# Two pairs of images in turn: the pieces of the front, the blocks of bins, and six buffers of head weights

## The chip, the cores and the metric

The kernel runs on one core of a Trainium2 chip. A core has five engines that each work through a queue of their own: PE (matrix products), DVE (VectorE), ACT (ScalarE), POOL (GpSimd) and SP, which here only issues transfers; 16 DMA engines move the data. The metric is the device time of one launch in microseconds (us), as a median over runs.

## The reference, cut to what matters

The input has 4 images of 48 x 48 positions and 128 channels. The first layer (a selective scan) is untouched by the change. The second layer is a spectral attention block; its input x1 is the first layer's output, and per image there are T = 48 tokens of 48 x 128 pixels.

```
xa_n = inorm(gn(x1))                       # group norm, then a norm per token
q, k, v = fno(xa_n; wQ), fno(xa_n; wK), fno(xa_n; wV)    # spectral convolution + skip, 32 heads
attn = softmax(q k^T / c)                  # per image and head: 48 x 48
out  = attn v                              # per head
projd = fno(out; wP)                       # spectral convolution + skip over the 32 heads
attention = inorm(projd + xa)
m = two more spectral layers on inorm(attention)
x = x1 + inorm(m) + attention
```

The kernel works with spectra: the value and the projection weights of a head are multiplied into one complex weight per bin and head, so that `attn v` and the projection become, for each block of bins, a sum over heads h and tokens s of attn[h, t, s] * (weight[h, bin] * spectrum[s, bin]). A complex product is made of three real ones (c = 0, 1, 2).

## The kernel before, in words

The instructions are laid on the engines' queues by a scheduler when the program is built. Those issued through the object `on` keep their program order on their engine (they all carry line 50 in the profile, the helper's line); those issued through `nc` may be moved where their data and buffers allow. A pool of tiles with `bufs=n` gives a tag n buffers in turn; a tile waits until the last reader of the buffer's previous tile is done. Pools that are closed give their memory to later ones.

The front of layer 1 handles the four images as two pairs. Per pair there are: `statistics` (12 `bn_stats`, two aggregates, then `group_affine`, a chain of small operations over DVE, PE and ACT); `first_norm`, a generator that yields after each piece (sums over positions with matmuls into `pm`, a normed image into `xa`, its square `sq`, and sums of squares with matmuls into `pv`); and `forward_w`, a generator that makes the transform along the width, six pieces of two matmuls `pa`, two evacuations to `a` and a store to DRAM (`da_x`). Before, pair 0 goes through all of it, then pair 1. Then come the combined head weights: `gw` on DVE, 12 steps of three transposes (`pgt`) into a PSUM bank and an ACT copy into `gtt`, and four stores into the DRAM tensor `dgt`. After that the spectra `a2` are read back and scaled, and `xa` is transposed (`pxn`).

The middle makes scores and softmax, and writes the tokens' spectra to the DRAM tensor `dxt` (`keys`).

The block loop follows. For each pair and each block k of 384 bins there are three accumulators in PSUM (`acc`, one set), and 12 groups (q, g): q counts 16 tokens, g counts 8 heads. A group takes `xrep` (spectra of 16 tokens, replicated over 8 heads, two transfers of 576 KB, new at each q, two buffers) and `grep` (weights of 8 heads, replicated over 16 tokens, one transfer of 576 KB, four per block, four buffers). ACT copies two thirds of `grep` to PSUM (line 1371), DVE multiplies it with `xrep` (line 1373), POOL multiplies the last third (line 1377), and PE sums with the attention weights `attn_c` (line 1381). At the end of a block ACT copies one accumulator (`s1`, line 1389), three DVE operations make `zt` (lines 1392 to 1394), and eight transposes (`pz`, line 1399) with two ACT copies write it to `z2`. Ahead of the loop stand 11 small loads of `wpv` and `mask`, four tiles `e_w` on DVE, and for each pair 48 matmuls (`pa`, line 1340) and a copy that give `a0_bd`, which is used only in the tail.

Of the kernel before, what the change touches and what calls it, by code (L numbers as in the profile page):

```python
# [10 lines left out]
F32 = mybir.dt.float32  # L11
# [4 lines left out]
PSUM = bass.MemoryType.PSUM  # L16
# [3 lines left out]
B, T, H, W = 4, 48, 48, 128  # L20
# [9 lines left out]
NH = 32  # L30
# [5 lines left out]
class Ordered:  # L36


    def __init__(self, tc):
        for name in ("tensor", "vector", "scalar", "gpsimd"):  # L40
            setattr(self, name, _OrderedEngine(tc, getattr(tc.nc, name)))
# [693 lines left out]
def layer1(ctx, tc, io, x1_dram, out):  # L735
# [5 lines left out]
    nc = tc.nc  # L741
# [10 lines left out]
    on = Ordered(tc)  # L752
# [48 lines left out]
    def statistics(psum, p, x):  # L801

        mv = small.tile([128, 2, 2], F32, tag=f"mv{p}", name=f"mv{p}", bufs=1)
        for b in range(2):
            st = small.tile([128, 6, 6], F32, tag="st", name=f"st1_{p}_{b}")
            for q in range(6):
                on.vector.bn_stats(st[:, q], x[:, b, q * HB : (q + 1) * HB].rearrange("p h t -> p (h t)"))
            on.vector.bn_aggr(mv[:, b], st)
        aff = small.tile([128, 2, 2], F32, tag=f"aff{p}", name=f"aff{p}", bufs=1)
        group_affine(on, small, psum, gmat, eps, mv[:, :, 0], mv[:, :, 1], aff[:, 0], aff[:, 1], 2, f"l1{p}")  # L810
        return aff

    def forward_w(psum, work, p, x, aff):


        da = dram.tile([2, 33, H, 96], F32, name=f"da_x{p}")
        fwa = work.tile([128, 2, 66], F32, tag="fwa", name=f"fwa{p}")
        for b in range(2):
            on.vector.tensor_scalar(fwa[:, b], fw, aff[:, 0, b : b + 1], None, ALU.mult)
        pb = psum.tile([128, 512], F32, tag="mm", name=f"pfwb{p}")  # L820
        on.tensor.matmul(pb[0:66, 0:2], fw, aff[:, 1], start=True, stop=True)
        fwb = small.tile([66, 2], F32, tag="fwb", name=f"fwb{p}")
        on.scalar.copy(fwb, pb[0:66, 0:2])
        for q in range(0, H, HB):
            a = work.tile([66, HB, 2, T], F32, tag="a", name=f"a_{p}_{q}")
# [12 lines left out]
        yield da  # L838

    def first_norm(psum, work, p, x, aff, y):  # L840
# [7 lines left out]
        def spread(t, name, more=False):  # L848

            v = small.tile([128, T], F32, tag="in_s", name=f"in_{name}{p}")  # L850
            on.vector.tensor_reduce(v, t[:, 0 : HB * T].rearrange("p (h t) -> p t h", t=T), AX.X, ALU.add)
            o = psum.tile([128, 512], F32, tag="st", name=f"po_{name}{p}", bufs=2)
            for b in range(2):
# [7 lines left out]

        pm = psum.tile([128, 512], F32, tag="st", name=f"pm{p}", bufs=2)
        for q in range(0, 24, HB):
# [15 lines left out]
        yield  # L879
        pv = psum.tile([128, 512], F32, tag="st", name=f"pv{p}", bufs=2)  # L880
        for i, b, h in quarters:
# [8 lines left out]
            )  # L890
            sq = work.tile([128, 24, T], F32, tag="sq", name=f"sq{p}_{i}")
            on.scalar.activation(sq, d, AF.Square)
# [25 lines left out]

    attn_c = pm.tile([128, B, 4, 3, 64], F32, name="attn_c")
    dxt = dram.tile([B, 4, T, 3 * NC], F32, name="dxt")  # L920

# [50 lines left out]
    def products():  # L972
# [5 lines left out]
        with ExitStack() as pw:  # L978
            q1 = pw.enter_context(tc.tile_pool(name="l1_v1", bufs=1))
            ps_t = pw.enter_context(tc.tile_pool(name="l1_vt", bufs=2, space=PSUM))  # L980

# [77 lines left out]
    with ExitStack() as ph:  # L1059
# [4 lines left out]
        rs, das = [], []  # L1064
        for p in range(2):
            aff = statistics(psst, p, x_in[p])
            norm = first_norm(psst, work, p, x_in[p], aff, xa)
            trans = forward_w(psum, work, p, x_in[p], aff)
            next(norm)
            next(trans)  # L1070
            next(norm)
            for _ in range(5):
                next(trans)
                next(norm)
            das.append(next(trans))
            rs.append(next(norm))
        with ExitStack() as pw:
            ps_t = pw.enter_context(tc.tile_pool(name="l1_wt", bufs=2, space=PSUM))
            q1 = pw.enter_context(tc.tile_pool(name="l1_w1", bufs=1, side="right"))
# [28 lines left out]
            for k in range(4):  # L1108
                gt = q1.tile([NH, 3, NC], F32, name=f"gtt{k}")
                for c in range(3):  # L1110
# [16 lines left out]
        for p in range(2):  # L1127
# [8 lines left out]

            p0 = psst.tile([128, 512], F32, tag="st", name=f"p0_x{p}", bufs=2)
            on.tensor.matmul(p0[0:H, 0:96], over_h, a2p[0:H, 0], start=True, stop=True)
# [48 lines left out]
        f32 = load("f32", [96, 24], io["c_F32"])  # L1187
        pu = psst.tile([128, 512], F32, tag="st", name="pu", bufs=2)
        nc.tensor.matmul(pu[0:24, 0:BT], f32, a2[:, 32], start=True, stop=True)
# [118 lines left out]
    with ExitStack() as ph:  # L1308
        p1 = ph.enter_context(tc.tile_pool(name="l1_q1", bufs=1))
        p2 = ph.enter_context(tc.tile_pool(name="l1_q2", bufs=2))  # L1310
        pg = ph.enter_context(tc.tile_pool(name="l1_qg", bufs=4))
        ps_t = ph.enter_context(tc.tile_pool(name="l1_qt", bufs=1, space=PSUM))
        ps_g = ph.enter_context(tc.tile_pool(name="l1_qp", bufs=2, space=PSUM))
        ps_y = ph.enter_context(tc.tile_pool(name="l1_qy", bufs=1, space=PSUM))


        wpv = p1.tile([128, 2, 4], F32, name="wpv")
        mask = p1.tile([128, 3, T], F32, name="mask")
        for c, n in enumerate(("wPs", "wVs")):
            w = io[n].rearrange("a b -> (a b)")  # L1320
            for g in range(4):
                nc.sync.dma_start(wpv[:, c, g : g + 1], w[8 * g : 8 * g + 8][None].to_broadcast([16, 8]))
        for q in range(3):
            nc.sync.dma_start(
                mask[:, q], io["c_ident"][16 * q : 16 * q + 16, 0:T][:, None].to_broadcast([16, 8, T])
            )
        nc.vector.tensor_mul(wpv[:, 0], wpv[:, 0], wpv[:, 1])
        e_w = []
        for g in range(4):
# [3 lines left out]
            e_w.append(e)  # L1333
        for pair in range(2):
            p = ps_t.tile([128, 512], F32, tag="tr", name=f"pa0{pair}")
# [12 lines left out]
            nc.scalar.copy(a0_bd[:, pair], p[0:96, 0:96])  # L1348
        for pair in range(2):
            for k in range(4):  # L1350
                acc = [ps_y.tile([128, 512], F32, tag=f"acc{c}", name=f"acc{pair}_{k}_{c}") for c in range(3)]
                gr = []
                for q in range(3):
                    x = p2.tile([128, 2, 3, NC], F32, tag="xrep", name=f"xrep{pair}_{k}_{q}")
                    for b in range(2):
                        nc.sync.dma_start(
                            x[:, b].rearrange("p c n -> p (c n)"),
                            dxt[2 * pair + b, k, q * 16 : q * 16 + 16][:, None].to_broadcast([16, 8, 3 * NC]),
                        )
                    for g in range(4):  # L1360
                        t = f"{pair}_{k}_{q}_{g}"
                        if q == 0:
                            r = pg.tile([128, 3, NC], F32, tag="grep", name=f"grep{t}")
                            nc.sync.dma_start(
                                r.rearrange("p c n -> p (c n)"),
                                dgt[k, 8 * g : 8 * g + 8][None].to_broadcast([16, 8, 3 * NC]),
                            )
                            gr.append(r)
                        r = gr[g]
                        gp = ps_g.tile([128, 2, 512], F32, tag="gp", name=f"gp{t}")  # L1370
# [8 lines left out]
                        for c in range(3):  # L1379
                            for b in range(2):  # L1380
# [6 lines left out]
                                )  # L1387
                s1 = p2.tile([128, NC], F32, tag="s1", name=f"s1{pair}_{k}")
                nc.scalar.copy(s1, acc[0][:, 0:NC])  # L1389
# [5 lines left out]
                for k4 in range(2):  # L1395
                    p = ps_t.tile([128, 512], F32, tag="tr", name=f"pz{pair}_{k}_{k4}")
                    for i in range(4):
# [6 lines left out]
                        p[0:96].rearrange("p (k b t) -> p k b t", b=2, t=64)[:, :, :, 0:T],  # L1404
                    )
    mid.close()

# [554 lines left out]
```

## Time and profile before

| | us |
|---|---|
| three runs | 5015.16, 5021.46, 5022.86; median 5021.46 |
| the profiled execution, time | 5017.78 |
| its span | 5016.0 |
| mean granted PE clock | 0.933 |

| stretch of the span | us | what runs in it |
|---|---|---|
| 0 to 4206 | 4206 | the first layer |
| 4206 to 4310 | 104 | the front of layer 1 |
| 4310 to 4445 | 135 | selection, scores, softmax, keys |
| 4445 to 4477.6 | 33 | entry of the block loop |
| 4477.6 to 4745 | 267 | the block loop, 8 blocks |
| 4745 to 5016 | 271 | the two spectral layers of the tail |

How to read it: the stretches are cut from the timeline of one execution, at the first `bn_stats` of layer 1 (4206.53), the last score matmuls, the first `acc` matmul (4477.62) and the last copies to `z2` (4744.45). The profile gives busy times of the engines in any stretch, the idle time before an instruction with the event that ended it, and a chain of waits followed back from the end. Matmul records come in pairs here: one issued product shows as two records or more.

### The profile page before, as it was taken

The numbers are of one execution on the slowest core, as the hardware profiler recorded it, in microseconds if no ns is written. First come the engines' busy times: TensorE is split into PE (matmuls) and PEld (weight loads), VectorE is DVE, ScalarE is ACT, GpSimd is POOL, SyncE is SP. The second block draws the span as 40 slices with busy tenths as digits, with TensorE's granted clock in tenths as the row PEclk, the third lists the DMA queues.
The fourth block names the chain that finished last, engine by engine and source line by source line (L and its number), as shares of the span: only waits on it lengthen the run. The fifth ranks groups of instructions, "written<-read, shape, count | busy, mean of one in ns | idle before, by whom it ended". The sixth has DMA issues, their size and how long they took to land.

```text
span 5016.0 us, 44268 instructions
## 1 busy us (share of the span) xinstructions
PE 4181.6 (83%) x12444; PEld 1916.5 (38%) x12444; DVE 4170.1 (83%) x2901; ACT 2953.2 (59%) x6608; POOL 3993.4 (80%) x2188
## 2 busy tenths in 40 slices
PE   6889898888798988887989888877788787888786
PEld 3334333333343333333433333333333332544443
DVE  3689998989899989898999898988999985556536
ACT  3666566766566666666666666665767663323334
POOL 4589998988899989898999898888999983246531
PEclk9989999999899999998999999998999998989877
DMA  2223232322232333232323332334333323147636
GB/s 54 74 89 101 91 116 89 104 89 97 92 107 94 116 89 104 88 102 90 106 95 117 92 102 91 98 101 96 106 106 102 103 91 88 40 97 172 160 99 151
DMA packets 278691, 501.01 MB, mean 100 GB/s; under 512 B 105940, under 2 KB 190036, under 8 KB 277868
## 3 DMA queue, kind: packets, MB, share of 16 engines
q1 hardware_dynamic: 272864, 495.11, 33.5%
q10 hardware_dynamic: 5580, 3.08, 0.2%
q8 instruction: 98, 1.61, 0.1%
q14 instruction: 149, 1.22, 0.1%
HBM read 462.93 MB, written 35.38 MB: 99 GB/s over the span
## 4 chain that ended last, share of the span: by engine, by line
DVE 17%; PE 15%; ACT 7%; issue 7%; POOL 3%; DMA 3%; SPq 1%; DVEq 0%; POOLq 0%; ACTq 0%
DVE h L50 12%; PE yp L50 4%; ACT da L50 3%; DVE db L50 3%; PE acc L1381 2%; POOL v L1377 1%; DMA grep<-dgt 1%; ACT L50 1%; PE sc L1254 1%; PE pi_p L50 1%; POOL db L50 1%; ACT dt L50 1%; POOL hc L50 1%; DVE m L50 1%; PE pe_m L50 0%
## 5 line engine op out<-in xcount | busy, mean ns | idle before, releaser
L50 POOL TENSOR_TENSOR hc<-h,cbc 128x960 f32<-128x960 f32 (+1 forms) x1280 | 2716.8, 2137 | 443.4 <-DVE h L50 328.5
L50 DVE TENSOR_TENSOR_SCAN h<-da,carry,db 128x961 f32<-128x961 f32 (+1 forms) x1280 | 2702.9, 2130 | 167.4 <-ACT carry L50 108.2
L50 ACT ACTIVATE da<-dt,a_neg 128x480 f32<-128x480 f32 (+1 forms) x2560 | 1660.9, 649 | 1188.1 <-DVE h L50 1143.2
L50 PE MATMUL yp<-hc,ident 128*128 128x480 f32 (+1 forms) x5120 | 2256.9, 568 | 19.4 <-POOL hc L50 19.2
L50 PEld LDWEIGHTS yp<-hc,ident 128*128 128x128 f32 x5120 | 999.1, 197 | 1381.4 <-issue 1003.7
L50 DVE TENSOR_TENSOR db<-du,pb 128x960 f32<-128x960 f32 (+1 forms) x960 | 1064.1, 1108 | 227.9 <-PE pb L50 172.0
L50 POOL TENSOR_TENSOR db<-du,bbc 128x960 f32<-128x960 f32 (+1 forms) x320 | 688.2, 2151 | 18.4 <-DMA bbc<-cd 9.6
L50 PE MATMUL pb<-bs,pick 112*128 112x480 bf16 (+1 forms) x960 | 357.7, 373 | 362.0 <-DVE db L50 360.3
L50 PE MATMUL pc<-pad,cdiag 128*128 128x480 f32 (+1 forms) x630 | 285.2, 564 | 8.3 <-ACT pad L50 8.3
L1377 POOL TENSOR_TENSOR v<-grep,xrep 128x768 f32<-128x768 f32 x96 | 174.4, 1819 | 117.9 <-PE acc L1381 60.8
L1381 PE MATMUL acc<-v,attn_c 128*64 128x384 f32 x1152 | 218.2, 513 | 36.5 <-ACT s L1389 32.1
L1373 DVE TENSOR_TENSOR v<-gp,xrep 128x1536 f32<-128x1536 f32 x96 | 168.1, 1757 | 88.7 <-PE acc L1381 41.3
L50 ACT COPY db<-carry 128x1 f32<-128x1 f32 x1280 | 226.0, 177 | 21.6 <-POOL db L50 15.1
L50 POOL TENSOR_TENSOR du<-dt,xc 128x480 f32<-128x480 f32 (+1 forms) x160 | 204.3, 1277 | 37.0 <-ACT dt L50 37.0
L50 PE MATMUL px<-xc,w_xp 128*112 128x480 f32 (+1 forms) x320 | 214.0, 756 | 16.9 <-ACT xc L50 13.3
L50 PEld LDWEIGHTS <-pick 112*128 112x128 bf16 x960 | 97.6, 102 | 329.1 <-issue 305.9
L50 ACT ACT_TABLE_LOAD x148 | 189.9, 1283 | 42.8 <-PE gv_l L50 19.5
L50 PE MATMUL pd<-xd,w_dt 8*128 8x480 f32 (+1 forms) x320 | 167.5, 603 | 40.5 <-ACT bs L50 24.7
L50 ACT COPY carry<-h 128x2 f32<-128x2 f32 x1024 | 192.6, 188 | 0.0
L50 PEld LDWEIGHTS pc<-pad,cdiag 128*128 128x128 f32 x630 | 122.6, 195 | 142.0 <-issue 115.5
L1371 ACT COPY gp<-grep 128x768 f32<-128x768 f32 x96 | 77.0, 803 | 157.3 <-DVE v L1373 79.7
L50 PE MATMUL yp<-y,ident 128*128 128x480 f32 (+1 forms) x240 | 167.6, 829 | 0.2
(366 smaller groups left out, 3162.5 us busy)
## 6 DMA issues: line engine op xcount, KB each, us to landing
cbc<-cd SPq DMA_DIRECT2D x512, 480.0 KB
bbc<-cd SPq DMA_DIRECT2D x256, 240.0 KB
cbc<-cd SPq DMA_DIRECT2D x128, 384.0 KB
xrep<-dxt SPq DMA_DIRECT2D x48, 576.0 KB
grep<-dgt SPq DMA_DIRECT2D x32, 576.0 KB
bbc<-cd SPq DMA_DIRECT2D x64, 192.0 KB
x<-in_xT SPq DMA_DIRECT2D x16, 288.0 KB
xr<-in_xT SPq DMA_DIRECT2D x16, 288.0 KB
```

The costliest lines, as they stand in the source:

```text
L50: return lambda *args, **kw: self._tc.keep_in_program_order(emit(*args, **kw))
L1254: nc.tensor.matmul(sc[64 * b : 64 * b + 64, g, 0 : 8 * T], qs[:, j, n, 2 * pair + b], f[b][:, 8 * g : 8 * g + 8], start=(jn == 0), stop=False,
L1371: nc.scalar.copy(gp[:, :, 0:NC], r[:, 0:2])
L1373: nc.vector.tensor_mul(v, gp[:, None, :, 0:NC].to_broadcast([128, 2, 2, NC]), x[:, :, 0:2])
L1377: nc.gpsimd.tensor_mul(v3, r[:, 2:3].to_broadcast([128, 2, NC]), x[:, :, 2])
L1381: nc.tensor.matmul(acc[c][64 * b : 64 * b + 64, 0:NC], attn_c[:, 2 * pair + b, g, q], v[:, b, c] if c < 2 else v3[:, b], start=first, stop ...
```

## The change

It has two halves, and some moves of memory.

In the front, statistics of both pairs are made first; those of pair 0 (`bn_stats` and aggregates) are issued through `nc`, so that they may be moved, while those of pair 1 keep their place. Then pieces of both pairs are issued in turn, pair 1 two pieces behind. The tags `a` and `sq` get three buffers, the tag `st` in PSUM three for two; to make room the pool of the transposed weights gets one bank for two, and `gtt` two buffers for four.

In the loop, blocks go k outside, pair inside, so that the weights of a block serve both pairs: 16 loads of `grep` for 32. They get six buffers. All loads of the loop go through `on.sync`, so SP sends them in program order, one step ahead. The loads of `wpv` and `mask` move ahead of the front. The mix of images of a pair moves into the loop, after block 1 of that pair.

```diff
-        for name in ("tensor", "vector", "scalar", "gpsimd"):
+        for name in ("tensor", "vector", "scalar", "gpsimd", "sync"):
...
-                on.vector.bn_stats(st[:, q], x[:, b, q * HB : (q + 1) * HB].rearrange("p h t -> p (h t)"))
-            on.vector.bn_aggr(mv[:, b], st)
+                (on if p else nc).vector.bn_stats(st[:, q], x[:, b, q * HB : (q + 1) * HB].rearrange("p h t -> p (h t)"))
+            (on if p else nc).vector.bn_aggr(mv[:, b], st)
...
-        for p in range(2):
-            aff = statistics(psst, p, x_in[p])
-            norm = first_norm(psst, work, p, x_in[p], aff, xa)
-            trans = forward_w(psum, work, p, x_in[p], aff)
-            next(norm)
-            next(trans)
-            next(norm)
-            for _ in range(5):
-                next(trans)
-                next(norm)
-            das.append(next(trans))
-            rs.append(next(norm))
+        affs = [statistics(psst, p, x_in[p]) for p in range(2)]
+        norms = [first_norm(psst, work, p, x_in[p], affs[p], xa) for p in range(2)]
+        trans = [forward_w(psum, work, p, x_in[p], affs[p]) for p in range(2)]
+        for i in range(9):
+            for p in range(2):
+                if 0 <= i - 2 * p < 7:
+                    if i - 2 * p == 0:
+                        next(norms[p])
+                    if i - 2 * p == 6:
+                        das.append(next(trans[p]))
+                        rs.append(next(norms[p]))
+                    else:
+                        next(trans[p])
+                        next(norms[p])
...
-            ps_t = pw.enter_context(tc.tile_pool(name="l1_wt", bufs=2, space=PSUM))
+            ps_t = pw.enter_context(tc.tile_pool(name="l1_wt", bufs=1, space=PSUM))
...
-                gt = q1.tile([NH, 3, NC], F32, name=f"gtt{k}")
+                gt = q1.tile([NH, 3, NC], F32, tag="gtt", name=f"gtt{k}", bufs=2)
...
-        pg = ph.enter_context(tc.tile_pool(name="l1_qg", bufs=4))
+        pg = ph.enter_context(tc.tile_pool(name="l1_qg", bufs=6))
...
+        steps = [(k, pair, q) for k in range(4) for pair in range(2) for q in range(3)]
+        xs, gs = {}, {}
+        def fetch_weights(k, some):
+            for g in some:
+                r = pg.tile([128, 3, NC], F32, tag="grep", name=f"grep{k}_{g}")
+                on.sync.dma_start(
+                    r.rearrange("p c n -> p (c n)"),
+                    dgt[k, 8 * g : 8 * g + 8][None].to_broadcast([16, 8, 3 * NC]),
+                )
+                gs[k, g] = r
+        def fetch(i):
+            if i == len(steps):
+                return
+            k, pair, q = steps[i]
+            x = p2.tile([128, 2, 3, NC], F32, tag="xrep", name=f"xrep{pair}_{k}_{q}")
+            for b in range(2):
+                on.sync.dma_start(
+                    x[:, b].rearrange("p c n -> p (c n)"),
+                    dxt[2 * pair + b, k, q * 16 : q * 16 + 16][:, None].to_broadcast([16, 8, 3 * NC]),
+                )
+            xs[i] = x
+            if i == 0:
+                fetch_weights(0, range(4))
+            elif pair == 1 and q == 2 and k < 3:
+                fetch_weights(k + 1, range(2))
+            elif pair == 0 and q == 0:
+                fetch_weights(k, range(2, 4))
+        fetch(0)
-        for pair in range(2):
-            for k in range(4):
+        for k in range(4):
+            for pair in range(2):
...
+                    i = steps.index((k, pair, q))
+                    fetch(i + 1)
+                    x = xs.pop(i)
...
+                        r = gs[k, g]
...
-                s1 = p2.tile([128, NC], F32, tag="s1", name=f"s1{pair}_{k}")
+                s1 = p2.tile([128, NC], F32, tag="s1", name=f"s1{pair}_{k}", bufs=1)
...
+                if k == 1:
+                    mix_of_images(pair)
```

`mix_of_images` is the old loop over the 48 matmuls of a pair and its copy, unchanged.

More of the change, by code (lines that the diff above doesn't have):

```diff
@@ L824, in forward_w @@
         for q in range(0, H, HB):
-            a = work.tile([66, HB, 2, T], F32, tag="a", name=f"a_{p}_{q}")
+            a = work.tile([66, HB, 2, T], F32, tag="a", name=f"a_{p}_{q}", bufs=3)
             for b in range(2):
@@ L851, in spread @@
             on.vector.tensor_reduce(v, t[:, 0 : HB * T].rearrange("p (h t) -> p t h", t=T), AX.X, ALU.add)
-            o = psum.tile([128, 512], F32, tag="st", name=f"po_{name}{p}", bufs=2)
+            o = psum.tile([128, 512], F32, tag="st", name=f"po_{name}{p}", bufs=3)
             for b in range(2):
@@ L860, in spread @@
             return o
-        pm = psum.tile([128, 512], F32, tag="st", name=f"pm{p}", bufs=2)
+        pm = psum.tile([128, 512], F32, tag="st", name=f"pm{p}", bufs=3)
         for q in range(0, 24, HB):
@@ L879, in first_norm @@
         yield
-        pv = psum.tile([128, 512], F32, tag="st", name=f"pv{p}", bufs=2)
+        pv = psum.tile([128, 512], F32, tag="st", name=f"pv{p}", bufs=3)
         for i, b, h in quarters:
@@ L890, in first_norm @@
             )
-            sq = work.tile([128, 24, T], F32, tag="sq", name=f"sq{p}_{i}")
+            sq = work.tile([128, 24, T], F32, tag="sq", name=f"sq{p}_{i}", bufs=3)
             on.scalar.activation(sq, d, AF.Square)
@@ L919, in layer1 @@
     attn_c = pm.tile([128, B, 4, 3, 64], F32, name="attn_c")
+    wpv = pm.tile([128, 2, 4], F32, name="wpv")
+    mask = pm.tile([128, 3, T], F32, name="mask")
+    for c, n in enumerate(("wPs", "wVs")):
+        w = io[n].rearrange("a b -> (a b)")
+        for g in range(4):
+            nc.sync.dma_start(wpv[:, c, g : g + 1], w[8 * g : 8 * g + 8][None].to_broadcast([16, 8]))
+    for q in range(3):
+        nc.sync.dma_start(
+            mask[:, q], io["c_ident"][16 * q : 16 * q + 16, 0:T][:, None].to_broadcast([16, 8, T])
+        )
+    nc.vector.tensor_mul(wpv[:, 0], wpv[:, 0], wpv[:, 1])
     dxt = dram.tile([B, 4, T, 3 * NC], F32, name="dxt")
@@ L979, in products @@
             q1 = pw.enter_context(tc.tile_pool(name="l1_v1", bufs=1))
-            ps_t = pw.enter_context(tc.tile_pool(name="l1_vt", bufs=2, space=PSUM))
+            ps_t = pw.enter_context(tc.tile_pool(name="l1_vt", bufs=1, space=PSUM))
             n_row = q1.tile([1, 2, 2, 128], F32, name="n_row")
@@ L1135, in layer1 @@
             on.scalar.copy(r_t[:, p : p + 1], pr[0:96, p : p + 1])
-            p0 = psst.tile([128, 512], F32, tag="st", name=f"p0_x{p}", bufs=2)
+            p0 = psst.tile([128, 512], F32, tag="st", name=f"p0_x{p}", bufs=3)
             on.tensor.matmul(p0[0:H, 0:96], over_h, a2p[0:H, 0], start=True, stop=True)
@@ L1187, in layer1 @@
         f32 = load("f32", [96, 24], io["c_F32"])
-        pu = psst.tile([128, 512], F32, tag="st", name="pu", bufs=2)
+        pu = psst.tile([128, 512], F32, tag="st", name="pu", bufs=3)
         nc.tensor.matmul(pu[0:24, 0:BT], f32, a2[:, 32], start=True, stop=True)
@@ L1314, in layer1 @@
         ps_y = ph.enter_context(tc.tile_pool(name="l1_qy", bufs=1, space=PSUM))
[L1317 to L1327, printed above, removed]
         e_w = []
@@ L1333, in layer1, with mix_of_images @@
             e_w.append(e)
-        for pair in range(2):
+        def mix_of_images(pair):
             p = ps_t.tile([128, 512], F32, tag="tr", name=f"pa0{pair}")
@@ L1348, in layer1 @@
             nc.scalar.copy(a0_bd[:, pair], p[0:96, 0:96])
-        for pair in range(2):
-            for k in range(4):
+        steps = [(k, pair, q) for k in range(4) for pair in range(2) for q in range(3)]
[8 more added lines that the diff above has]
+                gs[k, g] = r
@@ new lines, in fetch @@
+        def fetch(i):
[7 more added lines that the diff above has]
+                    dxt[2 * pair + b, k, q * 16 : q * 16 + 16][:, None].to_broadcast([16, 8, 3 * NC]),
+                )
+            xs[i] = x
[5 more added lines that the diff above has]
+                fetch_weights(k, range(2, 4))
@@ L1351, in layer1 @@
+        fetch(0)
+        for k in range(4):
+            for pair in range(2):
                 acc = [ps_y.tile([128, 512], F32, tag=f"acc{c}", name=f"acc{pair}_{k}_{c}") for c in range(3)]
-                gr = []
                 for q in range(3):
[L1354 to L1359, printed above, removed]
+                    i = steps.index((k, pair, q))
+                    fetch(i + 1)
+                    x = xs.pop(i)
@@ L1360, in layer1 @@
                     for g in range(4):
                         t = f"{pair}_{k}_{q}_{g}"
[L1362 to L1369, printed above, removed]
+                        r = gs[k, g]
```

## The prediction

> **What bounds the kernel now.** I read the table of busy time by stretch first. Up to 4180 us of the span the first layer runs; the diff does not touch it. It touches two stretches of the second layer: the front (4206 to 4310) and the block loop with its entry (4445 to 4745). The middle (4340 to 4445) and the tail (from 4745) keep their instructions, so I move them in time unchanged.
>
> The loop is 96 groups (2 pairs, 4 blocks of bins, 3 q, 4 g) of one ACT copy, one DVE multiply, one POOL multiply and 12 matmul records. Its chain of waits, with the entry (start, duration, what; us):
>
> ```profile
> 4452.23 8.76 DMA mask<-in_c_ident
> ...
> 4461.53 7.93 PE pa L1340 x48
> ...
> 4469.78 7.92 PE pa L1340 x48
> 4477.69 6.91 PE acc L1381 x26
> ...
> 4497.11 1.83 POOL v L1377
> 4498.96 9.00 DMA grep<-dgt
> ...
> 4508.78 0.48 ACT s L1389
> ...
> 4509.31 2.93 PE acc L1381 x7
> ```
>
> Before the first `acc` matmul stand a transfer of the mask and two mixes of images (`pa`). At each change of block stands a transfer of head weights: with four buffers, `grep` of the next block may start only when this block's last POOL multiply has let go. The same gap in the timeline of DVE (the bracket: idle before, and its releaser):
>
> ```profile
> 4566.71 1.76 DVE L1373 TENSOR_TENSOR v<-gp,xrep 128x1536 f32<-128x1536 f32 x1 [0.18 <-PE acc L1381]
> 4573.30 1.76 DVE L1373 TENSOR_TENSOR v<-gp,xrep 128x1536 f32<-128x1536 f32 x1 [4.83 <-ACT gp L1371]
> ...
> 4582.74 1.76 DVE L1373 TENSOR_TENSOR v<-gp,xrep 128x1536 f32<-128x1536 f32 x1 [3.22 <-PE acc L1381]
> 4585.40 1.76 DVE L1373 TENSOR_TENSOR v<-gp,xrep 128x1536 f32<-128x1536 f32 x1 [0.90 <-ACT gp L1371]
> ```
>
> Inside a block a multiply starts every 1.93 us, released by PE 0.18 us earlier: PE sets the pace, DVE (1.76) and POOL (1.82) sit just under it. Across a boundary 18.7 us pass from 4566.71 to 4585.40 in which four groups fit at 1.93. The busy times by stretch (PE, PEld, DVE, ACT, POOL with instruction counts; granted PE clock; DMA share; GB/s), first the end of one block:
>
> ```profile
> 4536.00:4540.00 4.00, 0.91 (x6) 0.14 (x2) 1.76 (x1) 0.80 (x1) 1.81 (x1) 1.00 1.00 235
> 4540.00:4544.00 4.00, 1.55 (x4) 0.30 (x4) 1.99 (x2) 1.99 (x3) 1.80 (x1) 0.53 1.03 240
> 4544.00:4548.00 4.00, 3.71 (x12) 1.33 (x12) 1.25 (x3) 1.11 (x3) 0.00 (x0) 0.62 0.99 229
> 4548.00:4552.00 4.00, 4.00 (x27) 2.16 (x25) 2.52 (x2) 1.47 (x3) 1.90 (x2) 1.00 0.04 10
> ```
>
> The 5.1 us without a matmul cost twice: PE stands, then restarts at half clock. And the front:
>
> ```profile
> 4217.50:4243.30 25.80, 23.15 (x86) 8.04 (x86) 10.78 (x16) 8.21 (x12) 0.00 (x0) 0.90 0.16 48
> 4243.30:4254.20 10.90, 1.17 (x5) 1.03 (x5) 8.62 (x27) 0.55 (x2) 0.00 (x0) 0.66 0.64 112
> 4254.20:4279.70 25.50, 23.35 (x100) 9.56 (x100) 10.66 (x16) 8.17 (x12) 0.00 (x0) 0.95 0.17 49
> ```
>
> Each pair's pieces are PE at 90%; between the pairs lies a stretch in which PE waits for the second pair's statistics.
>
> **The sum, part by part** (against the profiled execution, span 5016.0, time 5017.8).
>
> *1. Statistics of pair 0, free to move.* 12 `bn_stats` and two aggregates run from 4206.53 to 4212.80: 6.3 us. Through `nc` they may go into DVE's idle 17.3 us before 4201.74; their images had landed by 4195, when the transfer rate falls. Gain 6.3; at worst 0.
>
> *2. Pieces in turn.* Now: affine 0 4.6 us (4212.83 to 4217.4), pieces 27.3 (to 4244.7), statistics and affine of pair 1 9.5, pieces 27 (to 4281.1). After: affine 0 4.6, statistics and affine 1 9.5, since both are emitted ahead of any piece and stand in DVE's queue before `a_m`. Then all pieces. PE's own work is 23.2 + 22.1 us (the second without the `pxn` transposes that sat in its gaps), so 45.3 plus a 3 us tail (sum, root, reciprocal) = 48.3, against 54.3. Gain 6.0. With part 1: 12.3. Between no gain in the pieces (those of two pairs waiting on one another in fixed order) and 12.3 I take the upper end, because PE has under 3 us of idle per pair to lose.
>
> *3. One bank and two `gtt` buffers for the transposed weights.* The 12 steps of 3 transposes and a copy took from 4284.5 to 4294, 0.65 us apart in steady pace. With one bank a step is in series: about 0.6 PE + 0.47 ACT + two hand-overs of about 0.1 = 1.3 us, 12 x 0.65 = 7.8 more; two buffers make steps 7 to 12 wait for a store, 1 to 2 us more. Cover: the `pxn` transposes (14.2 us of PE), not pinned, which fill such gaps and otherwise come right after. I charge 2.3; without cover it is 9. Front: **-10**.
>
> *4. Mask and wpv early.* Eleven DMA issues of 0.6 us leave SP between 4445 and 4452.8. They go to SP's queue near 4196 ahead of the loads for `w_p`, `w_v`, first used at 4279: 6.6 us of delay there costs nothing. At the entry DVE's softmax tail was stuck 4.7 us behind `wpv`; `xrep` was issued at 4460.87 after that tail, so now at about 4456.
>
> *5. Entry without the mixes.* First `acc` matmul was 4477.6. Now SP sends, in fixed order, xrep 0 (two transfers), grep 0 to 3, xrep 1. One transfer of 576 KB at the loop's 242 GB/s is 2.44 us. Grep 0 lands at 4456 + 1.4 + 3 x 2.44 + 1.2 = 4466, the first matmul at about 4468.5; xrep 1, the eighth, at 4478, so group 5 at about 4480. Before, group 5 started near 4488 (four groups, the first 20 matmuls at half clock). **-8** (ends: -4 if the eight transfers share the queue and all land late, -10 if xrep 1 never stalls). The head weights that were sent at 4440.9, ahead of the entry, are now behind xrep 0: counted.
>
> *6. Seven boundaries.* Blocks 2 to 8 take (4739.9 - 4509.3) / 7 = 32.9 us. PE's need at full clock: 12 x 1.935 + 1.3 for two sets of `pz` transposes = 24.5. What stays is the evacuation of the single `acc` set: s1 copy 0.47, then three DVE operations of 0.55, with one 1.76 us multiply slotted between, before the last accumulator is free; from the last matmul that is 2.3 to 4.2 us, 3 taken. The next lateness is `xrep`: issued at 4553.76, its reader waited until 4561.05, 7.3 us for a step of 7.74, issued only when POOL frees the buffer. So slips of the 0.3 us seen before 4561.05 recur at steps, and where two greps (4.9 us) stand ahead on SP the next xrep is about 1.6 late, three times. Together 1 us per block. Block 28.5, gain 7 x 4.4 = **-31**. Fetching each weight once instead of twice takes 16 x 576 KB away; the remaining 9.44 MB per k last 39 us of 57, no bound.
>
> *7. The mixes in the loop.* 2 x 48 matmuls: 7.9 us each in the trace, at granted clock 0.50; half, 4, if warm. Partly they fill PE's wait for `acc`. Ends: 1 and 8 each; I take 3.5 each, **+7**.
>
> Two rules weighed. The page "TensorE: Matmul & The Clock Gate" (section on what is actually happening) says PE drops to half clock after an idle window of about 3.4 us and is released after one busy window of that length. The gap row agrees with the first half: 5.1 idle, then 0.53; a 3 us gap would stay warm. The second half fails here: PE was busy without a break from 4461.5 through the mixes, yet the clock stayed at 0.50 until 4481. By the rule the mixes cost 4 each, by the row 8 each with some 2 us of slow `acc` after: +8 or +20 without cover. That speaks against moving them into a warm loop, and is why I give no credit beyond cover. "DMA: Bandwidth & Descriptors" (Bandwidth, measured) has 1 MB in 6.15 us, 341 GB/s; the trace's replicated reads run at 242. By the page an estimate of 3.5 us for 1.18 MB would leave no slip; by the row 4.9 it slips, 7 us over the loop. I take the row.
>
> Sum: -10 - 8 - 31 + 7 = **-42**: profiled 4976. The median of the runs lies 3.7 above the profiled execution, so 4979.
>
> **Rivals.**
> (a) *Boundary stays cold* (15%): ACT's fixed order and the evacuation leave about 5 us without matmul, and half clock after. The row for: after 4573.30 the third multiply came 9.4 us later with three of its four weights landed. Against: part of that lateness is weights 2.4 us apart. Block 31: 7 x 1.9 = 13; mixes +10; -10 - 8 - 13 + 10 = -21, 5000.
> (b) *Boundary nearly closes* (22%): transposes and mixes fill PE's wait, block 26.5, mixes +2: -10 - 8 - 45 + 2 = -61, 4960.
> (c) *Front gives nothing* (13%): PE at 90% already, the bank of part 3 uncovered: +2 instead of -10, 4991. This is the case that the change's first half does not do what it says.
> (d) *Slower* (3%): the fixed order on SP becomes the bound. The first xrep pair took 9.9 us from issue to landing in a full queue. If each of 24 steps took that, and the 8 steps with weights 4.9 more, the loop would be 277 us from 4461, ending at 4738, mixes +16: 4754 against 4743, so 5030 with no front gain. It decides from 11.5 us a step; a lone xrep's 7.3 speaks against.
>
> Forecast 47%. A measurement here tells 0.2% (10 us) from no change. Range 4948 to 5003: takes (b), (c) and most of (a), leaving out (d) and the extremes. Faster 0.93, same 0.04, slower 0.03.
>
> **What would show it.** DVE statistics of pair 0 before 4202; PE without the 10 us hole between pairs; first `acc` at about 4468 less the front's 10; no `grep` in the chain at boundaries; clock near 1.0 there; block pitch 28.5; `pa` within the loop. Wrong if xrep heads the waits in most steps, if clock 0.5 follows each boundary, or if the stretch from pieces to `psel` (4313 before) ends no earlier.

## The result, and the profile after

The changed kernel takes 4989.17 us (median of 4 runs, 4987.73 to 4995.10) against 5021.93 (4 runs of the kernel before beside it, 5015.16 to 5022.86): a ratio of 0.994, 95% interval 0.9928 to 0.9953. That is 32.8 us where the forecast had 42. The profiled execution of the changed kernel is the slowest of its four, 4995.1 us with a span of 4993.3, so the traces differ by only 22.7 us; 3.7 of that goes the other way in the first layer, which the diff leaves alone. Behind the first layer the traces differ by 26.4 us.

Where it went, by stretches between marks that both kernels have (us; "first layer" ends with DVE's last operation on its output):

| stretch of the second layer | before | after | difference |
|---|---|---|---|
| end of first layer to the second pair's `in_r` (statistics, pieces) | 74.5 | 66.8 | -7.7 |
| to the first `p_x` (transposed head weights) | 12.7 | 20.8 | +8.1 |
| to the first `psel` | 19.7 | 21.3 | +1.6 |
| by way of the first `f` to the second pair's first maximum of the softmax (middle) | 131.7 | 134.8 | +3.1 |
| to the first `acc` matmul (entry) | 32.4 | 24.2 | -8.2 |
| to the first block's last `acc` matmul | 27.1 | 28.6 | +1.5 |
| to the eighth block's last `acc` matmul (seven boundaries and the mixes) | 236.5 | 216.8 | -19.7 |
| to the end (tail) | 274.8 | 269.7 | -5.1 |

The copy `s1` is no fair mark for a block's end. Before, ACT copied weights of the next block first and waited for them, so that `s1` of the first block came 4.1 us after its last `acc` matmul (4504.70); so it was in seven of eight blocks, by 3.0 to 4.6 us. After, it stands 1.2 us ahead of it in every block.

```profile
4508.04 0.80 ACT L1371 COPY gp<-grep 128x768 f32<-128x768 f32 x1 [1.65 <-DMA grep<-dgt]
4508.78 0.47 ACT L1389 COPY s<-acc 128x384 f32<-128x384 f32 x1
```

The front's first gain is given back one stretch later, so the whole net gain is the loop's, its entry's and its tail's. The changed kernel's chain of waits from the entry on (start, duration, what):

```profile
4467.32 11.45 DMA grep<-dgt
4480.71 25.50 PE acc L1407 x136
4525.05 10.56 DMA xrep<-dxt
4539.66 2.82 PE acc L1407 x4
...
4558.11 6.70 DMA xrep<-dxt
...
4568.91 1.50 PE acc L1407 x4
...
4573.79 4.21 PE pa L1343 x48
4589.71 9.97 DMA xrep<-dxt
...
4603.75 2.82 PE acc L1407 x4
```

The mask and the two cold mixes (met at half clock) ahead of the first `acc` are gone, and no `grep` heads a boundary any more. In its place stands `xrep`: 9.3 to 10.6 us where weights go with it, under 7 where they don't. Behind the long waits four `acc` matmuls take 2.82 us, behind the short ones 1.50. Busy time by stretch (PE, PEld, DVE, ACT, POOL, granted PE clock, DMA share, GB/s): pieces, transposed weights, the wait for the first transfers, then the second boundary in steps of 4 us:

```profile
4228.60:4276.90 48.30, 45.01 (x188) 17.16 (x188) 23.16 (x38) 17.26 (x26) 0.00 (x0) 0.95 0.30 77
4276.90:4298.00 21.10, 10.23 (x39) 3.82 (x40) 6.03 (x17) 5.51 (x12) 0.00 (x0) 0.52 0.17 36
4465.40:4478.20 12.80, 0.00 (x0) 0.00 (x0) 1.11 (x1) 1.23 (x2) 1.80 (x1) 0.50 0.91 210
...
4528.00:4532.00 4.00, 4.00 (x28) 1.75 (x26) 3.35 (x2) 1.90 (x3) 3.70 (x3) 1.00 1.04 233
4532.00:4536.00 4.00, 2.17 (x14) 0.72 (x10) 0.28 (x1) 0.85 (x2) 0.52 (x2) 1.00 1.00 226
4536.00:4540.00 4.00, 1.88 (x5) 0.62 (x6) 4.00 (x4) 0.80 (x1) 3.35 (x2) 0.64 1.05 236
4540.00:4544.00 4.00, 4.00 (x10) 1.40 (x10) 0.63 (x2) 1.26 (x2) 0.00 (x0) 0.51 0.85 194
```

The pieces take the 48.3 us that the forecast worked out, at 93% of PE. The stretch behind them had a mean granted clock of 0.78 before (4279.7 to 4295) and has 0.52 now. At the boundary DMA is full throughout, PE has its gap and then 10 matmuls in 4 us at half clock: the old picture, a little smaller. DVE's timeline at the same place, and at the front's affine above it (the bracket: idle before, and its releaser):

```profile
4217.27 0.16 DVE L932 TENSOR_TENSOR wpv<-wpv 128x4 f32<-128x4 f32 x1 [5.65 <-DMA mask<-in_c_ident]
4218.70 0.17 DVE L50 RECIPROCAL aff<-gs_l 128x2 f32<-128x2 f32 x1 [1.26 <-ACT gs_l L50]
...
4529.77 1.76 DVE L1399 TENSOR_TENSOR v<-gp,xrep 128x1536 f32<-128x1536 f32 x1 [0.18 <-PE acc L1407]
4535.73 1.76 DVE L1399 TENSOR_TENSOR v<-gp,xrep 128x1536 f32<-128x1536 f32 x1 [4.19 <-DMA xrep<-dxt]
...
4544.63 1.76 DVE L1399 TENSOR_TENSOR v<-gp,xrep 128x1536 f32<-128x1536 f32 x1 [3.54 <-PE acc L1407]
```

The `xrep` of block (k 1, pair 0) was issued at 4524.49 and its reader started at 4535.73, 11.2 us later. Laid out block by block, the distance from the last `acc` matmul of one block to that of the next shows where the loop still waits (us; the kernel of experiment 4 is beside it; the last column is the mean granted PE clock from the first to the eighth):

| kernel | to block 2 | 3 | 4 | 5 | 6 | 7 | 8 | clock |
|---|---|---|---|---|---|---|---|---|
| before | 32.2 | 34.2 | 34.5 | 33.1 | 34.1 | 34.2 | 34.1 | 0.91 |
| after | 27.3 | 33.0 | 32.1 | 36.7 | 27.5 | 32.8 | 27.4 | 0.95 |
| weights spread | 28.2 | 28.3 | 31.6 | 33.2 | 27.3 | 28.2 | 27.3 | 1.00 |

A boundary between the pairs of one k is the cheapest: 27.4 a block. One into a new k (blocks 3, 5, 7) costs about 5.5 more, and a block with a mix in it (4 and 5) about 4.3 more.

### The profile page after: what moved, and what is told of

Its sections match the earlier page's. It is cut to its first block, busy times and chain, and to the rows that moved or that the text cites. A ratio compares the mean times of both kernels' runs of the same rounds, so it can differ in the third digit from the quotient of the medians.

```text
span 4993.3 us, 44214 instructions
## 1 busy us (share of the span) xinstructions
PE 4171.9 (84%) x12444; PEld 1907.5 (38%) x12444; DVE 4168.5 (83%) x2901; ACT 2955.0 (59%) x6608; POOL 3993.1 (80%) x2188
## 4 chain that ended last, share of the span: by engine, by line
DVE 17%; PE 15%; issue 7%; ACT 7%; POOL 3%; DMA 2%; SPq 1%; DVEq 0%; POOLq 0%; ACTq 0%
DVE h L50 12%; PE yp L50 4%; ACT da L50 3%; DVE db L50 3%; PE acc L1407 2%; ACT L50 1%; PE sc L1270 1%; POOL v L1403 1%; DMA xrep<-dxt 1%; PE pi_p L50 1%; POOL db L50 1%; ACT dt L50 1%; DVE m L50 1%; PE po L50 1%; ACT ws L50 1%
## 5 line engine op out<-in xcount | busy, mean ns | idle before, releaser
L50 ACT COPY db<-carry 128x1 f32<-128x1 f32 x1280 | 226.0, 177 | 21.3 <-POOL db L50 13.9
L1407 PEld LDWEIGHTS acc<-v,attn_c 128*64 128x64 f32 x1152 | 111.5, 140 | 119.1 <-issue 64.3
```

The source lines that it names most:

```text
L50: return lambda *args, **kw: self._tc.keep_in_program_order(emit(*args, **kw))
L1407: nc.tensor.matmul(acc[c][64 * b : 64 * b + 64, 0:NC], attn_c[:, 2 * pair + b, g, q], v[:, b, c] if c < 2 else v3[:, b], start=first, stop ...
```

## The experiments

All ratios are against runs of the kernel before on the same chip (5019.3 to 5020.3 us by median), with 95% intervals; each kernel ran 4 or 5 times, the front alone 13 times. The experiments ran on three chips, so kernels of different experiments are compared by their ratios. These are known to about 0.13%, 6.5 us: repairs smaller than that are read from a stretch of one trace each. The loop itself scatters: in six kernels that have it as changed (the full change, the loop alone, the two of experiment 3, the two of experiment 2) it took 211.5 to 217.2 us between the last `acc` matmuls of the first and the eighth block.

**1. The front alone, and the loop alone.** The first keeps the changed front and has the old loop, with mask and `wpv` loaded where they were; the second has the old front and everything else new.

```diff
 # front alone
-        for k in range(4):
-            for pair in range(2):
+        for pair in range(2):
+            for k in range(4):
...
 # loop alone
-        affs = [statistics(psst, p, x_in[p]) for p in range(2)]
...
+        for p in range(2):
+            aff = statistics(psst, p, x_in[p])
```

> Front of the change, loop and entry of the kernel before (the mask's loads stay in the loop's entry). My theory: statistics moved into DVE's idle time and pieces in turn bring 12 us (the second in_r 67 us after the first layer's last DVE operation is replaced by about 62, before 74.5), and the single bank of the transposed weights takes back 8 to 9 of them (12 steps of 1.38 us for 0.65 to 0.8), so 5017 to 5020, 2 to 5 us under before. Rival: the fixed order of two pairs on one PE buys nothing by itself; then in_r is no earlier than 74 us and the time is 5028 or more.

> Loop and entry of the change, front of the kernel before. My theory: all of the 33 us come from here (entry 8, loop with its mixes 18, the rest small), so 4988 to 4996, the upper end if the product for wpv parks DVE in the front here too. Rival: the front carries a third of the gain; then 5000 or more.

Front alone: 5019.72 us, ratio 0.9998 (0.9989 to 1.0006). Loop alone: 4995.64, ratio 0.9954 (0.9942 to 0.9967). By itself the change's first half brings nothing that shows. Its trace says how: 64.0 us to the second `in_r` (-10.5), then 20.8 to `p_x` (+8.1) and 21.3 to `psel` (+1.6). It also shows that in the full change (66.8) something else takes 2.8 back, and the loop kernel shows the same with the old front: 82.9 where the kernel before has 74.5. What both have, and the front alone has not, are the early loads of mask and `wpv` with their product. So the halves do not simply add: with the early loads the old front loses 8.4 us, the new one 2.8. In the loop alone the product stands on DVE ahead of the statistics of pair 0 and holds them up:

```profile
4212.43 0.16 DVE L932 TENSOR_TENSOR wpv<-wpv 128x4 f32<-128x4 f32 x1 [6.95 <-DMA mask<-in_c_ident]
```

In the full change these statistics had moved ahead of it and were done at 4197.8.

**2. The front's lost 2.8 us.** DVE's first lines above suggest the product of `wpv`, which DVE meets in its queue ahead of the reciprocal and which waits 5.65 us for the small loads (the profile names the last of them, the mask). So the product alone was written late:

```diff
-    nc.vector.tensor_mul(wpv[:, 0], wpv[:, 0], wpv[:, 1])
...
+        nc.vector.tensor_mul(wpv[:, 0], wpv[:, 0], wpv[:, 1])
         e_w = []
```

> The changed kernel, but the one product of wpv is issued ahead of e_w instead of ahead of the front. My theory: DVE no longer stands 5.65 us in the middle of pair 0's affine chain waiting for the mask; ACT's part of that chain still needs 2 to 3 us, so 3 to 5 us less than the change: 4984 to 4986. Rival: the wait covered ACT's table load and root, which come anyway: 4989, no difference.

4993.3 us, ratio 0.9952 (0.994 to 0.9965), and 66.9 to `in_r`. A miss that decided nothing: the product isn't pinned, and the scheduler put it back in the same place (4214.30, 5.66 us idle before it). The second attempt moved the eleven loads too, and pinned the product behind the front:

```diff
-    for c, n in enumerate(("wPs", "wVs")):
...
-    nc.vector.tensor_mul(wpv[:, 0], wpv[:, 0], wpv[:, 1])
...
         products()
+        for c, n in enumerate(("wPs", "wVs")):
...
+        on.vector.tensor_mul(wpv[:, 0], wpv[:, 0], wpv[:, 1])
```

> The eleven small loads of wpv and mask and their product are written behind the front: on SP they now stand behind the six loads of w_p, w_v and the transform matrices, and DVE meets the product some 70 us later. If those early loads and the product are what took the front's missing 2.8 us (my account): ACT's root at the head of the affine no longer waits for the delayed store of the first layer, the stretch from the end of the first layer to the second in_r is 64.0 us as in the kernel with the front alone (66.8 in the changed kernel), and the whole kernel is 2.8 us faster than the changed one, some 4986. If the early loads cost nothing (the prediction's step), the stretch stays at 66.8 and the time at 4989.

64.0 us to `in_r`, as in the front alone. The whole kernel: 4987.17, ratio 0.9939 (0.9927 to 0.9952); by ratio no different from the changed kernel, so the stretch is the evidence. Who waits for the loads is seen on ACT's queue. The changed kernel, then this one:

```profile
4210.35 0.36 ACTq L469 DMA_DIRECT2D x<-ws  x1
4216.68 0.35 ACTq L772 DMA_DIRECT2D x_in<-x  x1
4217.11 1.28 ACT L50 ACT_TABLE_LOAD   x1 [17.72 <-POOL sel L983]
```

```profile
4210.57 0.35 ACTq L469 DMA_DIRECT2D x<-ws  x1
4214.21 0.36 ACTq L772 DMA_DIRECT2D x_in<-x  x1
4214.66 1.28 ACT L50 ACT_TABLE_LOAD   x1 [15.05 <-DMA x<-ws]
```

ACT stores the first layer's last piece and issues the load that reads it back; that issue waits for the store to land (the first bracket names `POOL sel`, which ended at 4216.81, behind the start of that issue; in the second kernel the issue goes out while `POOL sel` still works, until 4217.05). It waits 6.3 us in the changed kernel, where SP had sent eight of the small loads just ahead of the store and three behind it; 3.6 us here, with two ahead and one behind; and 3.5 in the front alone, with none. The table load and the root of pair 0's affine stand behind the issue in ACT's queue. So the product on DVE was not the only latecomer; ACT's root, which DVE's reciprocal needs, ended at 4218.7, later than the product. How small loads hold up a store, the traces do not show.

**3. The transposed head weights.** The stretch is 8.1 us longer. Is it the single bank, and why did the `pxn` transposes not cover it? The first kernel gives the weights three banks of the tag `st`, the second leaves the one bank and moves `r_t`, the scale that ACT needs to empty the `pxn` transposes, ahead of them.

```diff
 # three banks
-                    p = ps_t.tile([128, 512], F32, tag="tr", name=f"pgt{k}_{c}")
+                    p = psst.tile([128, 512], F32, tag="st", name=f"pgt{k}_{c}", bufs=3)
 # r_t first: written ahead of the pool l1_wt instead of behind it
+        for p in range(2):
+            on.tensor.matmul(pr[0:96, p : p + 1], rs[p][0:1], one1, start=True, stop=True)
+            on.scalar.copy(r_t[:, p : p + 1], pr[0:96, p : p + 1])
```

> The changed kernel, but the transposed weights use the three free banks of the sums in turn instead of the one bank. My theory: the 12 steps go from 1.38 us to 0.65 to 0.8 apart, 7 to 8 us earlier, and the stretch up to psel with them: 4981 to 4983. Rival: what follows waits for something else (spectra read back behind the stores of the weights, transposes pxn that PE must do anyway): less than 2 us, 4987 to 4989.

> The changed kernel, but the column r_t that scales the evacuation of the transposed images pxn is made ahead of the transposed weights instead of behind them. My theory: pxn stopped after 12 transposes because its three banks were full and ACT could not empty them without r_t, so PE stood 0.56 us in each of 12 steps at half clock; now pxn fills these gaps: 4 to 7 us less, 4982 to 4985. Rival: ACT, with 24 evacuations of 0.58 us, then comes between the steps of the weights and delays them by as much: 4988 to 4990.

Three banks: 4981.66 us, ratio 0.9929 (0.9916 to 0.9943); to `p_x` 12.3 instead of 20.8, then 19.7 to `psel` instead of 21.3. `r_t` first: 4983.7, ratio 0.9931 (0.9919 to 0.9944); to `p_x` 21.7, but from there to `psel` 12.5. PE's timeline before, in the changed kernel, with three banks, and with `r_t` first:

```profile
4286.84 6.77 PE L50 MATMUL pgt<-ident,gw 128*32 128x128 f32 x33 [1.55 <-DVE gw L50]
...
4294.94 8.74 PE L1151 MATMUL pxn<-ident,xa 128*96 128x128 f32 x60
```

```profile
4282.91 0.80 PE L50 MATMUL pgt<-ident,gw 128*32 128x128 f32 x3 [1.55 <-DVE gw L50]
4284.27 0.82 PE L50 MATMUL pgt<-ident,gw 128*32 128x128 f32 x3 [0.56 <-ACT gtt L50]
...
4299.30 6.46 PE L1167 MATMUL pxn<-ident,xa 128*96 128x128 f32 x32
```

```profile
4288.34 6.34 PE L50 MATMUL pgt<-ident,gw 128*32 128x128 f32 x33 [1.63 <-DVE gw L50]
```

```profile
4288.20 0.49 PE L50 MATMUL pgt<-ident,gw 128*32 128x128 f32 x3
4288.66 1.22 PE L1168 MATMUL pxn<-ident,xa 128*96 128x128 f32 x8
4289.71 0.49 PE L50 MATMUL pgt<-ident,gw 128*32 128x128 f32 x3
```

With one bank each step of three transposes waits for ACT's copy, a step takes 1.38 us, and no `pxn` stands between the steps: of its 96 records 12 come ahead of the steps and 84 after 4299. With three banks 33 transposes run without a break, as before. With `r_t` early `pxn` transposes, eight in most cases, sit in the gaps until all are done; only the last five steps wait again. The cover that the forecast named could not run: the banks of `pxn` stayed full since ACT couldn't empty them without `r_t`, which was pinned behind the weights that it was to cover. The trace before already showed it: there too PE stood idle for 1.55 us between the first steps with `pxn` waiting, and 84 of its 96 records came after the steps. Up to `psel` three banks bring 10 us of the front and `r_t` 8.

**4. The loop's weights.** One edit spreads the four weights of a new k: g 0 goes with step (pair 0, q 2), g 1 with (pair 1, q 0), and no longer both with (pair 1, q 2), just ahead of the two that follow the next `xrep`.

```diff
-            elif pair == 1 and q == 2 and k < 3:
-                fetch_weights(k + 1, range(2))
+            elif (pair, q) in ((0, 2), (1, 0)) and k < 3:
+                fetch_weights(k + 1, range(pair, pair + 1))
```

> The changed kernel, but of the next block's weights the two that need no released buffer are sent one at a time, two and three steps earlier, so that no two weights stand ahead of the xrep of the block's last step or of the next block's first. My theory: the queue is idle there, so the xrep that landed 11.2 us after issue at 4535.7 lands 7.3 us after it; PE no longer stands 3.5 us at these three changes of k nor restarts at half clock; three times 3.5 to 4 us: 4977 to 4979. Rival: the xrep itself sets the pace (7.3 us of 7.7), so a weight sent earlier delays another xrep by as much: 4987 to 4989.

4980.82 us, ratio 0.9927 (0.9914 to 0.9939); first to eighth block 204.0 us instead of 216.8, outside the scatter of 211.5 to 217.2. Its stretches and DVE lines at the same boundary:

```profile
4528.00:4532.00 4.00, 3.72 (x24) 1.38 (x20) 2.98 (x4) 1.42 (x3) 3.69 (x3) 1.00 1.03 250
4532.00:4536.00 4.00, 2.83 (x14) 1.05 (x12) 2.44 (x3) 1.84 (x3) 1.17 (x1) 1.00 1.03 244
4536.00:4540.00 4.00, 4.00 (x27) 2.22 (x25) 2.62 (x2) 1.38 (x3) 2.00 (x2) 1.00 0.25 64
```

```profile
4526.75 1.76 DVE L1399 TENSOR_TENSOR v<-gp,xrep 128x1536 f32<-128x1536 f32 x1 [0.18 <-PE acc L1407]
4529.53 1.76 DVE L1399 TENSOR_TENSOR v<-gp,xrep 128x1536 f32<-128x1536 f32 x1 [1.02 <-DMA xrep<-dxt]
```

At the three boundaries into a new k DVE waits 1.02, 0.38 and 1.06 us for `xrep` instead of 4.19, 3.16 and 2.93. PE's longest gap there is 1.2 us instead of 3.46, 2.43 and 2.20, its clock stays at 1.00 from the first block to the eighth, and the boundary is over some 5 us sooner. The table above has it for all three: 28.3, 33.2 (with a mix) and 28.2. The two weights behind the `xrep` were left where they are, so it is the two ahead of it that cost.

**5. The mixes.** They cost about 4.3 us a block in the loop. One kernel puts both mixes into the fourth k, one puts pair 0's at the entry, where PE waits 12.8 us for the first transfers.

```diff
 # late
-                if k == 1:
+                if k == 3:
 # at the entry
         fetch(0)
+        mix_of_images(0)
...
-                if k == 1:
+                if k == 1 and pair == 1:
```

> The changed kernel, but the mix of images of each pair comes after its last block (k = 3) instead of after k = 1. My theory: the first mix still costs about 4 us inside the loop (after block 3 of pair 0), the second falls behind the loop, where PE waits for transfers anyway: 3 to 4 us less, 4985 to 4986. Rival: its cost only moves into the tail, where PE is on the path (7.7 us of pe_p follow at once): 4989.

> Pair 0's mix of images is written right after the first fetch, ahead of the loop; pair 1's stays behind its second block. PE stands some 12 us between the softmax's last transposes and the first acc matmul, waiting for xrep and grep. If that wait covers the mix even at half clock (7.9 us as in the kernel before): the first acc comes no later (24.1 us behind the last maximum), and the loop from the first to the eighth s1 gets 4.2 us shorter (216.8 to 212.6): 4985. If the mix at the entry isn't covered, the first acc comes 3 to 4 us later and the time stays at 4989. If it warms PE's clock, the first block (27.4 from first acc to first s1) gets 1 to 2 us shorter besides.

Late: 4996.4 us, ratio 0.9952 (0.9939 to 0.9966); the loop takes 214.2, the tail 275.1 instead of 269.7, since pair 1's mix now stands in the tail and takes 7.92 us at half clock (its chain of waits):

```profile
4726.11 7.92 PE pa L1343 x48
```

At the entry: 4992.75, ratio 0.9943 (0.9929 to 0.9956); the loop takes 208.5 us (the block without its mix 27.5 instead of 32.1), but the first `acc` comes 3.8 us later. PE's timeline at that entry:

```profile
4462.54 3.08 PE L1343 MATMUL pa<-attn_c,e_w 128*96 128x48 f32 x18
4465.42 0.87 PE L1308 MATMUL pat<-ident,sn 128*128 128x128 f32 x3
4466.08 3.65 PE L1343 MATMUL pa<-attn_c,e_w 128*96 128x48 f32 x22
4469.53 0.87 PE L1308 MATMUL pat<-ident,sn 128*128 128x128 f32 x3
4470.19 1.41 PE L1343 MATMUL pa<-attn_c,e_w 128*96 128x48 f32 x8
4483.02 1.55 PE L1408 MATMUL acc<-v,attn_c 128*64 128x384 f32 x4 [11.42 <-POOL v L1404]
```

The scheduler put 40 of the 48 matmuls ahead of the softmax's last transposes. The first `xrep` is issued 0.07 us after those end (4465.31 and 4465.39 in the changed kernel, 4470.40 and 4470.47 here), so the wait that was to cover the mix began late, 4.1 us later if both are counted from the last maximum. Neither place shows a gain over the loop's middle by itself.

**6. Together.** First the late product, three banks, spread weights and `r_t` first; then also the late loads and pair 0's mix at the entry.

> Four edits at once on the changed kernel: product of wpv late, three banks for the transposed weights, the two weights sent singly and earlier, r_t first. My theory: 4 + 8 + 11 and about 1 more for r_t, which shares its gain with the banks: 4965 to 4968. Rival theories: without the loop's part 4976; without the front's 4977.

> All repairs in one kernel: transposed weights in three banks, r_t ahead of them, one block's weights sent one step at a time, early loads and product behind the front, pair 0's mix ahead of the loop. If the gains add (4970.7 measured with three of them, less 2.8 for the loads and 4.2 for the mix): 4963 to 4964, ratio 0.989. If the repairs overlap (loads late or mix at the entry worth nothing beside the others): 4967 to 4971.

4970.65 us, ratio 0.9906 (0.9892 to 0.9919), and 4963.51 (4960.47 to 4970.82), ratio 0.9893 (0.988 to 0.9907). The last is 57 us under the kernel before on its chip and, by ratio, some 24 under the change; these two are clear of the scatter. The stretches show what added: to `in_r` 63.9, from there to `psel` 33.0 (42.1 in the change, 32.4 before), and the loop 198.1. Banks and `r_t` overlap, as both mend the same 20 us: three banks alone have 32.0. The mix's entry gives back 2.6 of the 4 us that the loop gains.

## Why the prediction was right, and where it was wrong

| step | forecast | in the traces |
|---|---|---|
| 1, 2: statistics early, pieces in turn | -12.3 | -10.5 alone, -7.7 with step 4 |
| 3: one bank, two `gtt` buffers | +2.3 | +8.1, and +1.6 to `psel` |
| 4: early mask and `wpv` | 0 | +2.8, inside the -7.7 |
| 5: entry | -8 | -8.2 to the first `acc`, -6.7 to the end of the first block |
| 6: seven boundaries | -31 | -28.2 |
| 7: mixes in the loop | +7 | +8.5 |
| middle, tail | 0 | +3.1, -5.1 |

The measured 32.8 lies inside the forecast range, and as near to 42 as it is in part by luck. Between the two traces the gain is 26.4: the loop with its entry gained 26.4 of the 32 that were forecast (-8, -31, +7), the front lost 2.0 where it was to gain 10, and a tail 5.1 shorter, which was not forecast, made up for the front and a middle 3.1 longer. One sign that the prediction named for being wrong came true: `psel` started no earlier, at 4319.28 against 4313.54, of which 3.7 are the first layer's.

**Steps 1 and 2** held in mechanism: statistics of pair 0 at 4191.52 to 4197.8, no hole between pairs, 48.3 us of pieces. The 1.8 us missing even alone are, by the trace, ACT's: in the front alone its root is held to 5.2 us past the first layer's end by the issue of the last image, as in experiment 2. Before, that load was issued at 4208.80, while the statistics ran, and ACT's part of the affine was not due until 4215.24: the wait was hidden.

**Step 4** failed at "6.6 us of delay there costs nothing". The loads left SP not near 4196 but from 4205.42 to 4214.0, around the first layer's last store (4210.35). The step asked who needs the loads that stand behind on SP, and not whose transfer runs beside them: that store and, behind it, ACT's queue. The product on DVE, which unpinned instructions let into the affine, wasn't priced at all.

**Step 3** named the cost without cover, 9, and then charged 2.3 because `pxn` would fill the gaps. Measured 9.7. The error is the cover, not the price: experiment 3 shows that `pxn` could not run there. With steps 1 to 4 the front nets +2.0; rival (c), front gives nothing, had that number while the loop still gained. Its bank without cover was right; its other reason, that PE at 90% leaves the pieces nothing, was not, since they gave 10.5 alone. The step's own bound was the better number.

**Step 5** was right: its first reader met the first `grep` 10.9 us after the first `xrep` issue (10 forecast), and the first `acc` came after 12.9 (12.5 forecast). The fifth group gained 6.7 us, counted from the last maximum of the softmax, against 8.

**Step 6** was right in mechanism and short in one term. The base was 27.5 a block and the loop has 27.4 where no weights go. The slip was put at 1 us a block, 7 in all; measured, three boundaries of 5.5, 16. The text had the cause ("where two greps stand ahead on SP the next xrep is about 1.6 late"), but the size was low: `xrep` came 4.19, 3.16 and 2.93 us late, and with the two weights moved away (experiment 4) 1.02, 0.38 and 1.06. It also left out what such a lateness does: PE stood 3.46, 2.43 and 2.20 us and restarted at half clock each time, though the prediction's reading of the clock's rule was that "a 3 us gap would stay warm". Experiment 4 takes 12.9 of the 16 away. That -28.2 is still near -31 is luck of the mark: the old pitch was taken as 32.9 from the first `acc` matmul of block 2 to the last `s1`, where it is 33.8 from last `acc` to last `acc`. Rivals (a) and (b) were each right for some boundaries: within a k it nearly closes (27.4), into a new k it stays cold (33).

**Step 7**: 4.2 to 4.3 us each, 8.5 for both with what they delay. Of the two weighed numbers that of the rule (the Trainium skill, "TensorE: Matmul & The Clock Gate", on what is actually happening) was right for a mix met warm (granted clock 1.00 throughout, 4.28 us), and the old row's 7.9 for one met cold: the late kernel of experiment 5 has both, 4.28 and 7.92. The credit for cover, half a microsecond each, was not there. The 341 GB/s of the skill's page "DMA: Bandwidth & Descriptors" (Bandwidth, measured) did not show: replicated reads ran at 226 to 250 in the loop's full stretches, so the trace's row was the one to take. (1 MB in 6.15 us, as the page has it beside the 341, would be about 170 GB/s, so its two columns do not agree, and 3.5 us for 1.18 MB is an estimate from one of them alone.)

Middle and tail were moved unchanged and were not: for the middle see below. In the tail PE had half clock for 148.1 us before and for 138.8 after. Over the traces the tail goes along with that time: 269.6 to 270.9 us with 137 to 142, 272.0 to 272.8 with 141 to 145, 274.6 and 274.8 in the two kernels with the old loop, with 151 and 148 (the kernel with a mix in its tail left out). Why the half clock is shorter behind the new loop was not tried and stays open.

## What to carry to other kernels

Work that is to hide a cost must be able to run in that place: follow its operands and its buffers, up to the engine that empties them, before it is credited. Where transfers share one queue in fixed order, count what passes ahead of the next one that is read, and spread it over steps that have slack; what was 3 to 4 us late there cost 5.5, since PE came back at half clock. And moving a load early was not free while the previous stage's last store was in flight. To compare two loops, take a mark that waits for the same thing in both.

## What the runs showed of the hardware

Half clock can come without any long idle stretch, and the same code can get it or not. The changed kernel and the one with late loads run the same PE instructions in the middle, but one takes 1.4 us longer there at a lower clock. First the changed kernel, then the other, from their first `f` on, in steps of 2 us:

```profile
4346.20:4348.20 2.00, 1.04 (x9) 0.84 (x10) 1.99 (x2) 0.47 (x1) 1.39 (x2) 1.00 0.00 0
4348.20:4350.20 2.00, 1.20 (x4) 0.31 (x5) 2.00 (x2) 0.00 (x0) 2.00 (x1) 0.79 0.51 119
4350.20:4352.20 2.00, 2.00 (x8) 0.71 (x6) 2.00 (x2) 0.47 (x1) 0.33 (x1) 0.50 0.00 0
```

```profile
4343.30:4345.30 2.00, 1.07 (x9) 0.85 (x10) 2.00 (x2) 0.44 (x1) 1.43 (x2) 1.00 0.00 0
4345.30:4347.30 2.00, 1.20 (x6) 0.34 (x6) 2.00 (x2) 0.00 (x0) 2.00 (x1) 1.00 0.52 119
4347.30:4349.30 2.00, 2.00 (x14) 0.84 (x11) 2.00 (x2) 0.47 (x1) 0.58 (x2) 1.00 0.00 0
```

PE was busy for half of the first 4 us in both, with no idle stretch over 0.81 us, and lost its clock in one of them: the next 16 matmuls took 4.3 us there and 2.80 here. All 13 traces fall into two groups: from the first `f` to the first maximum it takes 48.2 us in five of them and 49.6 to 49.7 in eight, and only the eight have a half clock there, of 3.4 us, starting 3.1 to 3.4 us after the first `f`. A second such place lies before the second pair's first maximum: there the half clock lasted 6.8 us before and 10.2 in the changed kernel. Counted to there from the first `f`, the kernel before took 105.4 us and the changed one 107.8, so 2.4 of the middle's 3.1 us are the clock's.

At the boundaries into a new k the same holds for gaps. Eight traces have the changed order of weights, 24 such boundaries, with PE idle for 1.5 to 3.9 us at a stretch. A half clock of 3.4 or 6.8 us followed in 22; it did not after gaps of 1.46 and 2.02 us, but did after one of 1.80. What decides is not shown.
